# A fused adapter and layernorm on one core: the reciprocal deviation by one Heron step, squares taken from the sum, and fewer batches with b2 on the matrix engine

## The chip, the cores and the metric

The kernel runs on one core of a Trainium2 chip. The core has five engines that work side by side: TensorE (PE in the profile), VectorE (DVE), ScalarE (ACT), GpSimd (POOL) and SyncE (SP, which here only issues transfers). Each takes its instructions in the order in which they were written for it and waits for others through semaphores. The metric is the device time of one execution in microseconds; the median of three runs of the kernel before is 320.1 us (319.36 to 320.46).

## The reference, cut to what matters

The input x has 128 batches of 128 rows and 512 columns. Each batch b has a language id v (one of ten), which picks the adapter's weights and the norm's parameters. All is float32.

```python
h       = relu(x @ W1[v] + b1[v])            # 512 -> 128
adapted = h @ W2[v] + b2[v]                  # 128 -> 512
y       = x + adapted
mean    = y.mean(-1);  var = ((y - mean) ** 2).mean(-1)
out     = x + (y - mean) * rsqrt(var + 1e-5) * gamma[v] + beta[v]
```

## The kernel before, in words

All tables lie in SBUF for the whole run: the weights of all ten languages, and beta, gamma and b2, each spread over 128 partitions by a matmul at the start (`spread`, L157). For that, and for adding b2 later, the tables' 30 rows are held in bf16 as three parts that add up to the float32 value (`parts`), and a column of `pick` (L126) holds ones in the three places of one row.

One batch is one tile of 128 rows by 512 columns. It goes through these steps:

- `transpose_x` (PE, L197) and `copy_xT` (ACT, L201): x turned, by way of PSUM.
- `stage_w1` (ACT, L192): the language's W1 copied to a fixed place. `down` (PE, L220) and `relu` (ACT, L228): the hidden layer.
- `up` (PE, L237): the second product, into one of five PSUM buffers `ys[b]`. Where `b2_by_matmul(b)` holds (L187: the first four batches, and then each fourth), a bf16 matmul ahead of it (L236) puts b2[v] there first. Elsewhere `add_b2` (POOL, L207) has added b2 to x in a buffer r, one of four.
- `add_beta` (POOL, L214): x + beta into the output tile o of a pair of batches, one of five.
- `residual` (DVE, L243): y = ys + r (or + x), in PSUM; the row sums come out through DVE's accumulator, which a second small instruction reads. `negative_mean` (L248): -sum/512.
- `square` (ACT, L255): (y - mean) squared and summed. After each second batch `deviation` (L261): the square root.
- `rstd_1` to `rstd_5` (DVE, L264 to L281), once for a pair: a reciprocal of ACT's root and one Newton step for the reciprocal square root.
- `scale` (DVE, L287): (y - mean) times gamma[v], in place. `finish` (DVE, L296): times rstd, plus o. `store` (SP): 512 KB of a finished pair.

The order is written out by hand. A loop over i (L461) issues, for each engine, its steps for different batches: transposes of batch i, `down` and `relu` of i-1, `up` of i-2, `residual` of b = i-3, and `scale`, rstd steps and `finish` for the pair before b's. `keep` (L43) ties each instruction behind the one before it on its engine, so the program's order is each engine's order. The loop's body has two forms: b even (L494) and b odd (L509). On DVE, for an even b: residual, scale, negative_mean, rstd_1, rstd_2, finish, rstd_3; for an odd b: residual, rstd_4, scale, rstd_5, negative_mean, finish. Where an instruction of DVE reads what DVE has just written, it waits on DVE's own semaphore.

A language id is needed as a register where it picks a column range. `lid` (L171) loads four ids at a time on each engine; the loads of the following group are issued at the end of the loop's body (L525), for DVE behind the last `finish` of every fourth batch.

The last five batches, after E = 123, are issued by `tail` (L360), one by one instead of by pairs: `rstd_of` (L311) holds the same five steps for one batch, and `by_pool` (L342) gives three of the closing steps to ACT and POOL, for two of them with `shift` (L338, mean times rstd, on DVE) ahead. At b = E POOL gets the remaining b2 and beta additions in one go (L487).

Of the kernel before, what the change touches and what calls it, by code (L numbers as in the profile page):

```python
# [8 lines left out]
FP = mybir.dt.float32  # L9
# [7 lines left out]
P = 128  # L17
# [6 lines left out]
def cond_resid_kernel(ctx: ExitStack, tc: tile.TileContext, x, itok, W1, b1, W2, b2, gamma, beta, out):  # L24
# [102 lines left out]
    both = st.tile([P, R], FP, tag="both", name="both", bufs=1)[:96, :]  # L127
    keep(nc.vector.tensor_tensor(both, ident[:96, 0:R], ident[:96, 32 : 32 + R], ALU.add))
    keep(nc.vector.tensor_tensor(pick, both, ident[:96, 64 : 64 + R], ALU.add))


    wrap = const.tile([1, B], I32, name="wrap")
# [51 lines left out]
        return lids[g, engine][b % G]  # L184

    def b2_by_matmul(b):
        return b < 4 or b % 4 == 1  # L187

    def stage_w1(b):
        w1s[b] = wp.tile([P, KC, A], FP, tag="w1s", name=f"w1s_{b}")  # L190
# [39 lines left out]
    def up(b):  # L230
# [6 lines left out]
        keep(nc.tensor.matmul(ys[b], lhsT=hT[b], rhs=w2[:, bass.ds(v * H, H)], start=not m, stop=True))  # L237
        del hT[b]

    def residual(b):  # L240
        r = xb(b) if b2_by_matmul(b) else rs.pop(b)
        s = st.tile([P, 1], FP, tag="sum", name=f"sum_{b}")
        keep(nc.vector.scalar_tensor_tensor(ys[b], ys[b], 1.0, r, ALU.mult, ALU.add, accum_out=s))  # L243
        sums[b] = s

    def negative_mean(b):
        nmeans[b] = st.tile([P, 1], FP, tag="nmean", name=f"nmean_{b}")
        keep(nc.vector.tensor_scalar(nmeans[b], sums.pop(b), -1.0 / H, None, ALU.mult))  # L248

    def square(b):  # L250
        g, j = divmod(b, 2)
        if j == 0:
            ssqs[g] = st.tile([P, 2], FP, tag="ssq", name=f"ssq_{g}")
        sq = tp.tile([P, H], FP, tag="sq", name=f"sq_{b}")
        keep(nc.scalar.activation(sq, ys[b], AF.Square, bias=nmeans[b], accum_out=ssqs[g][:, j : j + 1]))  # L255

    sds, y0s, stats = {}, {}, {}

    def deviation(g):
        sds[g] = st.tile([P, 2], FP, tag="sd", name=f"sd_{g}")  # L260
        keep(nc.scalar.activation(sds[g], ssqs[g], AF.Sqrt, bias=eps, scale=1.0 / H))  # L261


    def rstd_1(g):  # L264
        stats[g] = p_s.tile([P, 6], FP, tag="s", name=f"stat_{g}")
        keep(nc.vector.tensor_scalar(stats[g][:, 0:2], ssqs.pop(g), -0.5 / H, -0.5 * EPS, ALU.mult, ALU.add))  # L266

    def rstd_2(g):
        y0s[g] = st.tile([P, 2], FP, tag="y0", name=f"y0_{g}")
        keep(nc.vector.reciprocal(y0s[g], sds.pop(g)))  # L270

    def rstd_3(g):
        keep(nc.vector.tensor_tensor(stats[g][:, 2:4], stats[g][:, 0:2], y0s[g], ALU.mult))  # L273

    def rstd_4(g):
        keep(nc.vector.tensor_tensor(stats[g][:, 4:6], stats[g][:, 2:4], y0s[g], ALU.mult))  # L276

    def rstd_5(g):
        rstds[g] = st.tile([P, 2], FP, tag="rstd", name=f"rstd_{g}")
        keep(  # L280
            nc.vector.scalar_tensor_tensor(rstds[g], stats.pop(g)[:, 4:6], 1.5, y0s.pop(g), ALU.add, ALU.mult)  # L281
        )

    def scale(b):
        v = lid(b, ET.DVE)
        keep(
            nc.vector.scalar_tensor_tensor(  # L287
                ys[b], ys[b], nmeans.pop(b), gamma_b[:, bass.ds(v * H, H)], ALU.add, ALU.mult
            )
        )  # L290

# [19 lines left out]
    def rstd_of(b, n):  # L311

        if not ends:
            ends["t"] = p_s.tile([P, 32], FP, tag="s", name="stat_ends")
        t = ends["t"][:, 8 * (b % 4) : 8 * (b % 4) + 3]
        if n == 1:
            keep(nc.vector.tensor_scalar(t[:, 0:1], ssqs.pop(b), -0.5 / H, -0.5 * EPS, ALU.mult, ALU.add))  # L317
        elif n == 2:
            y0s[b] = st.tile([P, 1], FP, tag="y0", name=f"y0_{b}")
            keep(nc.vector.reciprocal(y0s[b], sds.pop(b)))  # L320
        elif n < 5:
            keep(nc.vector.tensor_tensor(t[:, n - 2 : n - 1], t[:, n - 3 : n - 2], y0s[b], ALU.mult))  # L322
        else:
            rstds[b] = st.tile([P, 1], FP, tag="rstd", name=f"rstd_{b}")
            keep(nc.vector.scalar_tensor_tensor(rstds[b], t[:, 2:3], 1.5, y0s.pop(b), ALU.add, ALU.mult))  # L325

    def deviation_of(b):
        ssq = st.tile([P, 1], FP, tag="ssq", name=f"ssq_{b}")
        sq = tp.tile([P, H], FP, tag="sq", name=f"sq_{b}")
        keep(nc.scalar.activation(sq, ys[b], AF.Square, bias=nmeans[b], accum_out=ssq))  # L330
        sds[b] = st.tile([P, 1], FP, tag="sd", name=f"sd_{b}")
        keep(nc.scalar.activation(sds[b], ssq, AF.Sqrt, bias=eps, scale=1.0 / H))
        ssqs[b] = ssq

    def rstd_col(b):
# [1 line left out]

    def shift(b):  # L338
        ends[b] = st.tile([P, 1], FP, tag="shift", name=f"shift_{b}")
        keep(nc.vector.tensor_tensor(ends[b], nmeans.pop(b), rstd_col(b), ALU.mult))  # L340

    def by_pool(b, scaled):  # L342

# [16 lines left out]
    def tail(b):  # L360
        p = E // 2
        if b == E + 3:
            rstd_of(b - 2, 4)
        residual(b)
        if b == E + 1:
            rstd_1(p)
            rstd_2(p)
            negative_mean(b)
            rstd_3(p)
            scale(E - 1)  # L370
            rstd_4(p)
            rstd_5(p)
            shift(E)
            finish(E - 2)
            store(p - 1)
            deviation_of(b)
            by_pool(E, False)
        elif b == E + 2:
            negative_mean(b)
            rstd_of(b - 1, 1)  # L380
            rstd_of(b - 1, 2)
            finish_last(E - 1)
            store_last(E)
            rstd_of(b - 1, 3)
            deviation_of(b)
        elif b == E + 3:
            rstd_of(b - 2, 5)
            negative_mean(b)
            shift(b - 2)
            residual(b + 1)  # L390
            negative_mean(b + 1)
            by_pool(b - 2, False)
            store_last(b - 2)
            rstd_of(b - 1, 1)
            rstd_of(b - 1, 2)
            rstd_of(b - 1, 3)
            scale(b - 1)
            deviation_of(b)
            rstd_of(b - 1, 4)
            rstd_of(b - 1, 5)  # L400
# [6 lines left out]
            rstd_of(b + 1, 1)  # L407
            rstd_of(b + 1, 2)
            rstd_of(b, 3)
            rstd_of(b + 1, 3)  # L410
            scale(b + 1)
            rstd_of(b, 4)
            rstd_of(b + 1, 4)
            rstd_of(b, 5)
            rstd_of(b + 1, 5)
            finish_last(b)
            finish_last(b + 1)

# [42 lines left out]
    for i in range(3, B + U):  # L461
        if i < B and i % G == 0 and i // G + 3 < NG:
            load_x(i // G + 3)
        b = i - U - 1
        if i == 4:
            up(2)
        if i > 3 and on(i):
            transpose_x(i)
        if b <= E:
            add_b2(b + 2)  # L470
            add_beta(b)
        if i > 4 and on(i - 1):
# [12 lines left out]
        p = g - 1  # L485
        mine, old = 0 <= p < B // 2, 0 <= p - 1 < B // 2
        if b == E:  # L487
            for n in range(b + 3, B):
                add_b2(n)
            for n in range(b + 1, B):  # L490
                add_beta(n)
        if b > E:
            tail(b)
        elif half == 0:  # L494
            if on(b):
                residual(b)
            if mine:
                scale(2 * p)
            if on(b):
                negative_mean(b)  # L500
            if mine:
                rstd_1(p)
                rstd_2(p)
            if old:
                finish(2 * p - 1)
                store(p - 1)
            if mine:
                rstd_3(p)
        else:  # L509
            if on(b):  # L510
                residual(b)
            if mine:
                rstd_4(p)
                scale(2 * p + 1)
                rstd_5(p)
# [49 lines left out]
```

## Time and profile before

| | |
|---|---|
| median of three runs | 320.1 us |
| profiled execution: its time, its span | 319.72, 318.0 us |
| granted clock of TensorE | 0.99 |
| PE, DVE, ACT, POOL busy | 302.7, 297.9, 289.1, 280.6 us |
| batches with b2 by matmul (L236) | 35, 0.38 us each |
| additions on POOL: b2 (L207), beta (L214) | 93, 128; 1.28 us each |
| scale (L287), finish (L296), residual (L243) on DVE | 0.75, 0.74, 0.69 us each |
| one rstd step (L266, L270, L273, L276, L281) | 0.15 to 0.21 us, 62 of most |

The span is the time from the first to the last instruction of the profiled execution. Instructions of an engine overlap: the next can start before the one in front has put away its last results. So in a timeline the distance from one start to the next tells what an instruction costs its engine, and the duration tells when others can use its result. The ends of matmuls are modelled, and a busy PE is not PE at its peak; there too the distances between starts are what is read.

### The profile page before, as it was taken

How to read it: one execution, taken by the hardware profiler on the slowest of the kernel's cores; microseconds unless marked ns; L12 is line 12 of the kernel's file. 1: busy time of each engine (PE TensorE's matmuls, PEld its weight loads, DVE VectorE, ACT ScalarE, POOL GpSimd, SP SyncE). 2: the span in 40 equal slices, each digit the busy share in tenths (PEclk: the TensorE clock that was granted, in tenths of full speed). 3: DMA queues.
4: the chain of work that ended last, by engine and by line, in shares of the span. 5: the costliest groups of instructions: out<-in, count | busy, mean ns of one | idle time of the engine just before them, and what ended most of it. 6: DMA issues, size and time to landing. Idle time of an engine off the chain costs nothing. (4 is left out here: it accounts for less than half of the span.)

```text
span 318.0 us, 7173 instructions
## 1 busy us (share of the span) xinstructions
PE 302.7 (95%) x1883; PEld 225.0 (71%) x1884; DVE 297.9 (94%) x995; ACT 289.1 (91%) x726; POOL 280.6 (88%) x234
## 2 busy tenths in 40 slices
PE   7989999999999999999999999999999999999950
PEld 3566777777777777777777777777777777777730
DVE  6827999999999999999999999999999999999995
ACT  3977999999999999999999999999999999999971
POOL 1308999999999999999999999999999999999873
PEclk9999999999999999999999999999999999999995
DMA  7998777667776666677776666677766666633333
GB/s 204 318 386 294 205 260 262 233 232 266 260 242 212 215 223 242 228 238 265 261 231 215 209 227 248 223 245 264 258 220 208 222 231 241 219 128 133 132 128 138
DMA packets 41002, 72.88 MB, mean 229 GB/s; under 512 B 1753, under 2 KB 6884, under 8 KB 40962
## 3 DMA queue, kind: packets, MB, share of 16 engines
q1 hardware_dynamic: 40902, 72.38, 67.2%
q8 instruction: 15, 0.25, 0.3%
q14 instruction: 25, 0.20, 0.2%
q10 hardware_dynamic: 60, 0.05, 0.1%
HBM read 38.86 MB, written 33.55 MB: 228 GB/s over the span
## 5 line engine op out<-in xcount | busy, mean ns | idle before, releaser
L214 POOL TENSOR_TENSOR o<-x,beta_b 128x512 f32<-128x512 f32 x128 | 162.1, 1280 | 9.2 <-ACT beta_b L164 9.2
L207 POOL TENSOR_TENSOR r<-x,b_b 128x512 f32<-128x512 f32 x93 | 118.9, 1279 | 20.2 <-DMA x<-in_x_dram 12.3
L220 PE MATMUL ph<-xT,w1s 128*128 128x128 f32 x1024 | 135.6, 275 | 0.7 <-ACT w1s L192 0.5
L237 PE MATMUL py<-w,hT 128*128 x256 | 131.0, 594 | 0.9 <-DMA w<-in_L_cond_W_dram 0.7
L220 PEld LDWEIGHTS ph<-xT,w1s 128*128 128x128 f32 x1024 | 124.6, 192 | 2.8 <-ACT hT L228 1.4
L197 PEld LDWEIGHTS pxT<-ident,x 128*128 128x128 f32 x512 | 63.7, 140 | 66.1 <-issue 45.3
L287 DVE SCALAR_TENSOR_TENSOR py<-py,nmean,gamma_b 128x512 f32<-128x512 f32 x126 | 94.6, 751 | 0.0
L255 ACT ACTIVATE sq<-py,nmean 128x512 f32<-128x512 f32 x124 | 85.3, 688 | 6.7 <-DVE nmean L248 4.2
L296 DVE SCALAR_TENSOR_TENSOR o<-py,rstd,o 128x512 f32<-128x512 f32 x122 | 90.3, 740 | 1.0
L192 ACT COPY w1s<-w 128x512 f32 x128 | 79.5, 622 | 0.2 <-DMA w<-in_L_cond_W_dram 0.2
L201 ACT COPY xT<-pxT 128x512 f32<-128x512 f32 x128 | 73.8, 577 | 5.1 <-PE pxT L197 3.6
L197 PE MATMUL pxT<-ident,x 128*128 128x128 f32 x512 | 76.8, 273 | 0.7 <-ACT xT L201 0.7
L243 DVE SCALAR_TENSOR_TENSOR py<-py,r 128x512 f32<-128x512 f32 x93 | 64.4, 692 | 2.5 <-PE pxT L197 0.9
L228 ACT ACTIVATE hT<-ph,b1T 128x128 f32<-128x128 f32 x128 | 47.6, 372 | 1.2 <-PE ph L220 1.2
L237 PEld LDWEIGHTS py<-w,hT 128*128 128x128 f32 x256 | 41.6, 192 | 4.0 <-issue 2.0
L243 DVE SCALAR_TENSOR_TENSOR py<-py,x 128x512 f32<-128x512 f32 x35 | 24.1, 690 | 4.9 <-PE py L237 4.8
L255 ACT ACTIVATION_READ_ACCUMULATOR sq<-py,nmean 128x1 f32 x124 | 24.8, 200 | 0.0
L261 ACT ACTIVATE sd<-ssq,eps 128x2 f32<-128x2 f32 x62 | 18.3, 296 | 2.1
L248 DVE TENSOR_SCALAR nmean<-sum 128x1 f32<-128x1 f32 x128 | 18.7, 146 | 0.2
L236 PE MATMUL py<-parts,pick 96*128 96x512 bf16 x35 | 13.3, 381 | 0.0
L243 DVE DVE_READ_ACCUMULATOR py<-py,r 128x1 f32 x93 | 13.0, 140 | 0.0
L276 DVE TENSOR_TENSOR stat<-stat,y 128x2 f32<-128x2 f32 x62 | 12.7, 205 | 0.0
(54 smaller groups left out, 113.7 us busy)
## 6 DMA issues: line engine op xcount, KB each, us to landing
out_dram<-o SPq DMA_DIRECT2D x61, 512.0 KB, 3.6
x<-in_x_dram SPq DMA_DIRECT2D x30, 1024.0 KB, 6.0
w<-in_L_cond_W_dram SPq DMA_DIRECT2D x4, 640.0 KB, 6.6
w<-in_L_cond_W_dram SPq DMA_DIRECT2D x2, 1280.0 KB, 11.3
x<-in_x_dram SPq DMA_DIRECT2D x4, 512.0 KB, 8.5
out_dram<-o SPq DMA_DIRECT2D x6, 256.0 KB, 2.4
rows<-in_L_cond_beta_dram ACTq DMA_DIRECT2D x1, 20.0 KB
rows<-in_L_cond_gamma_dram SPq DMA_DIRECT2D x1, 20.0 KB
```

The source lines that it names most:

```text
L192: keep(nc.scalar.copy(w1s[b].rearrange("p k a -> p (k a)"), src))
L197: keep(nc.tensor.transpose(pxs[b][:, k, :], xb(b)[:, k * P : (k + 1) * P], ident))
L201: keep(nc.scalar.copy(xT[b], pxs.pop(b)))
L207: keep(nc.gpsimd.tensor_tensor(rs[b], xb(b), b2_b[:, bass.ds(v * H, H)], ALU.add))
L214: keep(nc.gpsimd.tensor_tensor(os[g][:, j, :], xb(b), beta_b[:, bass.ds(v * H, H)], ALU.add))
L220: nc.tensor.matmul(phs[b], lhsT=w1s[b][:, k, :], rhs=xT[b][:, k, :], start=(k == 0), stop=(k == KC - 1))
L228: keep(nc.scalar.activation(hT[b], phs.pop(b), AF.Relu, bias=b1T[:, bass.ds(lid(b, ET.Activation), 1)]))
L237: keep(nc.tensor.matmul(ys[b], lhsT=hT[b], rhs=w2[:, bass.ds(v * H, H)], start=not m, stop=True))
L243: keep(nc.vector.scalar_tensor_tensor(ys[b], ys[b], 1.0, r, ALU.mult, ALU.add, accum_out=s))
L255: keep(nc.scalar.activation(sq, ys[b], AF.Square, bias=nmeans[b], accum_out=ssqs[g][:, j : j + 1]))
L287: nc.vector.scalar_tensor_tensor(ys[b], ys[b], nmeans.pop(b), gamma_b[:, bass.ds(v * H, H)], ALU.add, ALU.mult)
L296: nc.vector.scalar_tensor_tensor(o, ys.pop(b), rstds[g][:, j : j + 1], o, ALU.mult, ALU.add)
```

## The change

Four things are changed together.

- **Heron's step.** With s the root from ACT and a the exact variance plus eps, the kernel now forms s + a/s, which is twice the improved root, and takes its reciprocal. That is four DVE instructions for a pair instead of five: reciprocal, (ssq + eps) times it, that plus s, reciprocal. The result is half of the reciprocal deviation, so gamma's columns of `pick` are doubled once at the start, and with them the spread gamma.
- **Square from the sum.** `square` takes the row sum as its bias and -512 as its scale, so that it squares sum - 512 y, which is 512 times the distance from the mean. It reads `sums` and no longer `nmeans`; the constants 1/512^3 take the factors out again. Sums and negative means lie in tiles of two columns, one pair each.
- **b2 by matmul** in the first four batches and then in batches 1, 6 and 11 of each sixteen, instead of each fourth: 27 batches instead of 35. The other 8 are added on POOL.
- **Order on DVE.** For an even b: residual, scale, rstd_1, negative_mean, rstd_2, finish, rstd_3. For an odd b: residual, rstd_4, negative_mean, scale, finish. The tail is arranged anew, and in POOL's last block the addition of b2 to the last batch moves behind the beta additions.

```diff
+    keep(nc.vector.tensor_scalar(pick[:, L : 2 * L], pick[:, L : 2 * L], 2.0, None, ALU.mult))
...
-        return b < 4 or b % 4 == 1
+        return b < 4 or b % 16 in (1, 6, 11)
...
+    def col(tiles, b):
+
+        return tiles[b // 2][:, b % 2 : b % 2 + 1]
+
     def residual(b):
         r = xb(b) if b2_by_matmul(b) else rs.pop(b)
-        s = st.tile([P, 1], FP, tag="sum", name=f"sum_{b}")
-        keep(nc.vector.scalar_tensor_tensor(ys[b], ys[b], 1.0, r, ALU.mult, ALU.add, accum_out=s))
-        sums[b] = s
+        if b % 2 == 0:
+            sums[b // 2] = st.tile([P, 2], FP, tag="sum", name=f"sum_{b // 2}")
+        keep(
+            nc.vector.scalar_tensor_tensor(ys[b], ys[b], 1.0, r, ALU.mult, ALU.add, accum_out=col(sums, b))
+        )
...
-        keep(nc.scalar.activation(sq, ys[b], AF.Square, bias=nmeans[b], accum_out=ssqs[g][:, j : j + 1]))
+        keep(
+            nc.scalar.activation(
+                sq, ys[b], AF.Square, bias=col(sums, b), scale=-float(H), accum_out=col(ssqs, b)
+            )
+        )
...
+    H3 = float(H) ** 3
...
-        keep(nc.scalar.activation(sds[g], ssqs[g], AF.Sqrt, bias=eps, scale=1.0 / H))
+        keep(nc.scalar.activation(sds[g], ssqs[g], AF.Sqrt, bias=eps, scale=1.0 / H3))
...
     def rstd_1(g):
-        stats[g] = p_s.tile([P, 6], FP, tag="s", name=f"stat_{g}")
-        keep(nc.vector.tensor_scalar(stats[g][:, 0:2], ssqs.pop(g), -0.5 / H, -0.5 * EPS, ALU.mult, ALU.add))
+        y0s[g] = p_s.tile([P, 6], FP, tag="s", name=f"stat_{g}")
+        keep(nc.vector.reciprocal(y0s[g][:, 0:2], sds[g]))
 
     def rstd_2(g):
-        y0s[g] = st.tile([P, 2], FP, tag="y0", name=f"y0_{g}")
-        keep(nc.vector.reciprocal(y0s[g], sds.pop(g)))
+        t = y0s[g]
+        keep(nc.vector.scalar_tensor_tensor(t[:, 2:4], ssqs.pop(g), EPS * H3, t[:, 0:2], ALU.add, ALU.mult))
 
     def rstd_3(g):
-        keep(nc.vector.tensor_tensor(stats[g][:, 2:4], stats[g][:, 0:2], y0s[g], ALU.mult))
+        t = y0s[g]
+        keep(nc.vector.scalar_tensor_tensor(t[:, 4:6], t[:, 2:4], 1.0 / H3, sds.pop(g), ALU.mult, ALU.add))
 
     def rstd_4(g):
-        keep(nc.vector.tensor_tensor(stats[g][:, 4:6], stats[g][:, 2:4], y0s[g], ALU.mult))
-
-    def rstd_5(g):
         rstds[g] = st.tile([P, 2], FP, tag="rstd", name=f"rstd_{g}")
-        keep(
-            nc.vector.scalar_tensor_tensor(rstds[g], stats.pop(g)[:, 4:6], 1.5, y0s.pop(g), ALU.add, ALU.mult)
-        )
+        keep(nc.vector.reciprocal(rstds[g], y0s.pop(g)[:, 4:6]))
...
         if b == E:
-            for n in range(b + 3, B):
-                add_b2(n)
+            add_b2(b + 3)
             for n in range(b + 1, B):
                 add_beta(n)
+            add_b2(b + 4)
...
             if mine:
                 scale(2 * p)
+                rstd_1(p)
             if on(b):
                 negative_mean(b)
             if mine:
-                rstd_1(p)
                 rstd_2(p)
...
             if mine:
                 rstd_4(p)
-                scale(2 * p + 1)
-                rstd_5(p)
             if on(b):
                 negative_mean(b)
             if mine:
+                scale(2 * p + 1)
                 finish(2 * p)
```

`rstd_of` for single batches changes in the same way. In `tail`, the four steps take the places of the five, with negative_mean moved between the reciprocal and the step that reads it, and the third and fourth steps of batch 124 around residual(126).

More of the change, by code (lines that the diff above doesn't have):

```diff
@@ L238, in up @@
         del hT[b]
+    def col(tiles, b):
+        return tiles[b // 2][:, b % 2 : b % 2 + 1]
     def residual(b):
         r = xb(b) if b2_by_matmul(b) else rs.pop(b)
-        s = st.tile([P, 1], FP, tag="sum", name=f"sum_{b}")
-        keep(nc.vector.scalar_tensor_tensor(ys[b], ys[b], 1.0, r, ALU.mult, ALU.add, accum_out=s))
-        sums[b] = s
+        if b % 2 == 0:
[3 more added lines that the diff above has]
+        )
     def negative_mean(b):
-        nmeans[b] = st.tile([P, 1], FP, tag="nmean", name=f"nmean_{b}")
-        keep(nc.vector.tensor_scalar(nmeans[b], sums.pop(b), -1.0 / H, None, ALU.mult))
+        if b % 2 == 0:
+            nmeans[b // 2] = st.tile([P, 2], FP, tag="nmean", name=f"nmean_{b // 2}")
+        keep(nc.vector.tensor_scalar(col(nmeans, b), col(sums, b), -1.0 / H, None, ALU.mult))
     def square(b):
@@ L287, in scale @@
             nc.vector.scalar_tensor_tensor(
-                ys[b], ys[b], nmeans.pop(b), gamma_b[:, bass.ds(v * H, H)], ALU.add, ALU.mult
+                ys[b], ys[b], col(nmeans, b), gamma_b[:, bass.ds(v * H, H)], ALU.add, ALU.mult
             )
@@ L316, in rstd_of @@
         if n == 1:
-            keep(nc.vector.tensor_scalar(t[:, 0:1], ssqs.pop(b), -0.5 / H, -0.5 * EPS, ALU.mult, ALU.add))
+            keep(nc.vector.reciprocal(t[:, 0:1], sds[b]))
         elif n == 2:
[L319 to L322, printed above, removed]
+            keep(
+                nc.vector.scalar_tensor_tensor(t[:, 1:2], ssqs.pop(b), EPS * H3, t[:, 0:1], ALU.add, ALU.mult)
+            )
+        elif n == 3:
+            keep(nc.vector.scalar_tensor_tensor(t[:, 2:3], t[:, 1:2], 1.0 / H3, sds.pop(b), ALU.mult, ALU.add))
         else:
             rstds[b] = st.tile([P, 1], FP, tag="rstd", name=f"rstd_{b}")
-            keep(nc.vector.scalar_tensor_tensor(rstds[b], t[:, 2:3], 1.5, y0s.pop(b), ALU.add, ALU.mult))
+            keep(nc.vector.reciprocal(rstds[b], t[:, 2:3]))
     def deviation_of(b):
@@ L329, in deviation_of @@
         sq = tp.tile([P, H], FP, tag="sq", name=f"sq_{b}")
-        keep(nc.scalar.activation(sq, ys[b], AF.Square, bias=nmeans[b], accum_out=ssq))
+        keep(nc.scalar.activation(sq, ys[b], AF.Square, bias=col(sums, b), scale=-float(H), accum_out=ssq))
         sds[b] = st.tile([P, 1], FP, tag="sd", name=f"sd_{b}")
-        keep(nc.scalar.activation(sds[b], ssq, AF.Sqrt, bias=eps, scale=1.0 / H))
+        keep(nc.scalar.activation(sds[b], ssq, AF.Sqrt, bias=eps, scale=1.0 / H3))
         ssqs[b] = ssq
@@ L339, in shift @@
         ends[b] = st.tile([P, 1], FP, tag="shift", name=f"shift_{b}")
-        keep(nc.vector.tensor_tensor(ends[b], nmeans.pop(b), rstd_col(b), ALU.mult))
+        keep(nc.vector.tensor_tensor(ends[b], col(nmeans, b), rstd_col(b), ALU.mult))
     def by_pool(b, scaled):
@@ L362, in tail @@
         if b == E + 3:
-            rstd_of(b - 2, 4)
+            rstd_of(b - 2, 3)
         residual(b)
@@ L366, in tail @@
             rstd_1(p)
+            negative_mean(b)
             rstd_2(p)
-            negative_mean(b)
+            scale(E - 1)
             rstd_3(p)
-            scale(E - 1)
             rstd_4(p)
-            rstd_5(p)
             shift(E)
@@ L378, in tail @@
         elif b == E + 2:
+            rstd_of(b - 1, 1)
             negative_mean(b)
-            rstd_of(b - 1, 1)
             rstd_of(b - 1, 2)
@@ L383, in tail @@
             store_last(E)
-            rstd_of(b - 1, 3)
             deviation_of(b)
         elif b == E + 3:
-            rstd_of(b - 2, 5)
-            negative_mean(b)
+            rstd_of(b - 2, 4)
             shift(b - 2)
             residual(b + 1)
-            negative_mean(b + 1)
             by_pool(b - 2, False)
@@ L394, in tail @@
             rstd_of(b - 1, 1)
+            negative_mean(b)
             rstd_of(b - 1, 2)
-            rstd_of(b - 1, 3)
+            negative_mean(b + 1)
             scale(b - 1)
             deviation_of(b)
+            rstd_of(b - 1, 3)
             rstd_of(b - 1, 4)
-            rstd_of(b - 1, 5)
             scale(b)
@@ L407, in tail @@
             rstd_of(b + 1, 1)
+            rstd_of(b, 3)
             rstd_of(b + 1, 2)
-            rstd_of(b, 3)
-            rstd_of(b + 1, 3)
             scale(b + 1)
             rstd_of(b, 4)
+            rstd_of(b + 1, 3)
             rstd_of(b + 1, 4)
-            rstd_of(b, 5)
-            rstd_of(b + 1, 5)
             finish_last(b)
@@ L513, in cond_resid_kernel @@
                 rstd_4(p)
-                scale(2 * p + 1)
-                rstd_5(p)
             if on(b):
```

## The prediction

> **What bounds the kernel now.** First the page's busy table and the sums of three stretches of the span:
>
> ```profile
> PE 302.7 (95%) x1883; PEld 225.0 (71%) x1884; DVE 297.9 (94%) x995; ACT 289.1 (91%) x726; POOL 280.6 (88%) x234
> ```
>
> ```profile
> 30.00:300.00 270.00, 270.00 (x1715) 205.25 (x1714) 266.42 (x901) 259.42 (x661) 262.06 (x213) 1.00 0.66 225
> ```
>
> Four engines lie within 4% of the stretch's length, so shares don't settle it; PE's is modelled too. What settles it is the rhythm, in PE's timeline:
>
> ```profile
> 155.44 0.60 PE L197 MATMUL pxT<-ident,x 128*128 128x128 f32 x4
> ...
> 157.63 0.60 PE L197 MATMUL pxT<-ident,x 128*128 128x128 f32 x4
> 158.07 1.06 PE L220 MATMUL ph<-xT,w1s 128*128 128x128 f32 x8
> 158.96 0.38 PE L236 MATMUL py<-parts,pick 96*128 96x512 bf16 x1
> 159.18 1.02 PE L237 MATMUL py<-w,hT 128*128 x2
> 160.04 0.60 PE L197 MATMUL pxT<-ident,x 128*128 128x128 f32 x4
> ```
>
> A batch takes 2.19 us from transpose to transpose (155.44 to 157.63), and 2.41 with a b2 matmul (157.63 to 160.04): 0.22 each. Four batches take 8.98, unbroken from 31 to 301 us: PE sets the pace. DVE's timeline shows how near it is:
>
> ```profile
> 153.72 0.69 DVE L243 SCALAR_TENSOR_TENSOR py<-py,r 128x512 f32<-128x512 f32 x1
> ...
> 154.99 0.15 DVE L248 TENSOR_SCALAR nmean<-sum 128x1 f32<-128x1 f32 x1
> 155.05 0.15 DVE L266 TENSOR_SCALAR stat<-ssq 128x2 f32<-128x2 f32 x1
> 155.11 0.15 DVE L270 RECIPROCAL y<-sd 128x2 f32<-128x2 f32 x1
> 155.18 0.73 DVE L296 SCALAR_TENSOR_TENSOR o<-py,rstd,o 128x512 f32<-128x512 f32 x1
> ...
> 155.89 0.69 DVE L243 SCALAR_TENSOR_TENSOR py<-py,r 128x512 f32<-128x512 f32 x1
> ...
> 157.42 0.75 DVE L296 SCALAR_TENSOR_TENSOR o<-py,rstd,o 128x512 f32<-128x512 f32 x1
> 158.22 0.70 DVE L243 SCALAR_TENSOR_TENSOR py<-py,r 128x512 f32<-128x512 f32 x1
> ```
>
> One pair (153.72 to 158.22) takes 4.50; the pair before (149.28 to 153.72) 4.44; together 8.94 against PE's 8.98. DVE's bound is 0.5% away. Small operations last 0.15 but follow each other at 0.06 to 0.07. The finish at 157.42 is followed by residual after 0.80, the one at 153.05 after 0.67. At the first place, once in four batches, stands the loading of the next four language ids into registers (L174). It takes no engine time, but DVE's instructions are handed out behind it. The answer by source line gives its length:
>
> ```profile
> L174 DVEq TENSOR_LOAD <-lang x32: 341/612/1049, 24.6 to 301.0; - x32
> ```
>
> The finish in front of it waits for rstd_5, so finish is handed out only when it can start, and the load starts with it. Finish alone would let residual go after 0.66; the load makes it 0.80, sticking out by 0.14. Where it took 1.05, at 49.26, residual came 1.23 after finish.
>
> [...] the ids are loaded while a finish handed out before runs on[...]. [...] Here such a wait costs: a reader starts 0.19 after the small writer's start (308.69 to 308.88 in the tail), not 0.07. [...] shift (L340), at 303.82, lasts 0.46, till POOL's additions end at 304.26.
>
> **The change part by part** (durations of the profiled execution: span 318.0, its time 319.72, 0.4 below the median of 320.1).
>
> *PE.* Picks fall from 35 to 27. Seven of the eight lie before residual(124): 7 x 0.22 = 1.54 off PE; batch 125 in the tail is the eighth. PE's four batches become 4 x 2.19 + 0.75 x 0.22 = 8.925.
>
> *POOL* takes 8 additions, at 1.23 start to start: +9.9. Sixteen batches need (13 + 16) x 1.23 = 35.7, PE 35.7. But POOL runs ahead: r_4 ends at 26.6 and its residual starts at 31.95, 5.3 later. The one addition that batch 5 now needs costs some 1.2 of this, later ones only keep POOL from gaining. Work on path: nil. Without the lead, 9.9 would appear. x buffers are freed later by the 2 to 4 us of lead that POOL lacks, and SP's queue holds its loads, and the stores behind them, as much longer. The load of group 8 is issued at 63.61, needs 6.0, and its first transpose is at 88.19: 18 us hide it. If that were gone, transposes would wait for x.
>
> *DVE, first half of a pair.* Now nmean, rstd_1, rstd_2, finish take 0.19 (154.99 to 155.18). New: reciprocal, nmean, rstd_2, which reads the reciprocal's result: 0.19 of waiting plus 0.07 to finish = 0.26. Loss 0.065, in both pairs 0.13 per four batches. Behind the waiting rstd_2 stand finish, rstd_3 and the next residual, and for that residual ACT's square waits, with 2 us of room until its deviation is used.
>
> *DVE, second half.* nmean now stands directly behind residual and rstd_4 and must wait for the accumulator. In the tail the same step is 308.39 (accumulator read) to 308.56: 0.17. scale stands behind it with its register instruction; the same pattern 308.88 to 309.01 is 0.13. So residual to finish: 0.61 + 0.17 + 0.13 + 0.67 = 1.58, against 1.53 (155.89 to 157.42) and 1.59 (151.46 to 153.05): loss 0.04. rstd_5 and its wait are gone from this place.
>
> *DVE, the ids.* finish now waits for rstd_4, written before scale, so it enters the queue while scale runs, and the load behind it can start some 0.65 earlier. Its excess vanishes; finish to residual becomes 0.66: -0.14 in one pair and -0.01 in the other, and another -0.01 for a residual that already stands in the queue. From scale's start to finish's end are 1.3 us: even a load of 1.05 nearly fits.
>
> Sum: 0.13 + 0.04 - 0.16 = 0.01: DVE stays at about 8.945, and is now just above PE's 8.925. Residual(3) starts at 29.68, PE-fed as today; residual(124) at 301.73: 272.05 for 121 batches. After: 30.25 x 8.945 = 270.6. Three long loads cost DVE 0.48, 0.41 and 0.39 today (at 50.47, 59.77 and 230.26, together 1.3), which its small lead over PE pays back; with no such lead I keep 0.5 of it: 271.1. Gain 1.0.
>
> *ACT.* square needs the sum only: 4.2 of waits for nmean are taken from an engine with 3% of room; nothing on the path. sqrt has equal form and cost.
>
> *Front.* One more small operation on pick, before DVE's wait of 0.4 for rows: hidden.
>
> *Tail*, DVE's own: residual(124) to the last pair of finishes is 301.73 to 313.11 = 11.38. One of the five rstd steps goes for each of five batches (two pairs and single ones), which is worth 0.07 where it was covered and 0.19 where the next one read it. Against that, both shifts, with two SBUF inputs, can be held by POOL, which now works on its additions until about 25.35 + 227 x 1.232 = 305.0 instead of 304.3. Between 10.6 (steps gained, 4 x 0.19) and 11.8 (nothing gained but a shift held 0.4 longer): I take 10.9, gain 0.5. The last r_127, at the end of POOL's block, is ready by 305; residual(127) wants it at about 306.5.
>
> Total -1.5: 320.1 - 1.5 = 318.6.
>
> Unknowns, both ends: the ids' load, -0.15 to 0 per four batches (0 = +4.2 on the sum); the two waits, 0.02 more or less each, four times per four batches: +-2.4; the tail, -0.8 to +0.4.
>
> **Rivals.** *PE alone decides*: DVE's waits are each 0.01 to 0.02 cheaper. Then 1.54 + tail 0.8 + the start: 317.4 to 317.8. For it: PE's floor is only 0.02 below; against: DVE's waits were measured.
>
> *The new waits eat it all*: DVE at 8.98 per four, 0.01 more per wait; 30.25 x 8.98 + 0.5 = 272.1; tail 0: 320.1. For it: the margin is thin; against: the long loads lose their exposed part.
>
> *Slower: the ids' load stays exposed.* If the sequencer can't pass finish before the engine takes it, 0.14 per four batches remains: 30.25 x 0.14 = 4.2, so 318.6 + 4.2 = 322.8. It decides from 0.05 per four batches on. For it: today every load starts with a finish; against: at 24.65 a load ran behind a small instruction and no finish at all, and today's finish is handed out late because it waits for rstd_5, a cause that goes.
>
> *Slower: POOL.* At 1.28 start to start instead of 1.23 it needs 37.1 per sixteen batches, 1.3 more than DVE, 10 in all, less its lead of 5: 323 to 325. Against: 1.23 was held through the whole catching-up at 31 to 100 us.
>
> **How the numbers follow.** As summed (317.9 to 319.1) 0.46; PE alone 0.14; nothing left (within 0.3%, about what a measurement of this kernel can tell from none, so 319.1 to 321.1) 0.22; ids' load 0.12; POOL 0.06. Faster 0.60, same 0.22, slower 0.18. The range, 317.2 to 321.3, leaves out the two slow rivals and the edge of the PE case. The likeliest case alone is 317.9 to 319.1.
>
> **What would show it.** Right: transposes 2.19 and 2.41 as before, but with waits of PE for DVE's finish (L309 of the new kernel) in the middle; four batches at 8.93 to 8.96; every finish followed by residual at 0.65 to 0.67, ids' loads beginning during scale; reciprocal to rstd_2 0.19; residual to finish 1.58. Wrong: residual waiting for POOL's r; loads still starting with finish; four batches above 8.98; or residual to finish well off 1.58.

## The result and the profile after

The changed kernel takes 330.84 us (median of six runs, 330.49 to 331.53), against 320.1 before: 1.0343 times as long, with an interval of 1.0326 to 1.036. The prediction was 318.6, with a range of 317.2 to 321.3. The profiled execution took 330.74 us, its span is 329.0. Ratios and intervals, here and below, are from undisturbed executions; one kernel of the experiments, the one before with the new picks and kept stores, ran some 2% longer in five of its eight executions, for a reason that stays open, and is read by the other three. First the page's busy table of the changed kernel, and the sums of the same long stretch of its span (the last three columns are TensorE's granted clock, the DMA share and GB/s):

```profile
PE 305.1 (93%) x1876; PEld 224.7 (68%) x1876; DVE 308.8 (94%) x930; ACT 288.1 (88%) x726; POOL 289.6 (88%) x242
```

```profile
30.00:300.00 270.00, 268.49 (x1693) 202.93 (x1692) 267.09 (x831) 256.07 (x656) 259.11 (x211) 1.00 0.65 224
```

The table says little. PE is busy 2.4 us more though it has eight matmuls less; DVE is busy 10.9 us more though it has 65 instructions less, mostly because the table counts an operation that is held up as busy (7.96 of the shift below). In the long stretch POOL is busy 2.95 us *less* than before (262.06), although it was given more to do. The landmarks in DVE's timeline tell more:

| | before | predicted | after |
|---|---|---|---|
| residual(3) starts | 29.68 | as before | 30.02 |
| DVE, four batches | 8.94 | 8.945 | 9.01 |
| residual(124) starts | 301.73 | 300.8 | 305.19 |
| from there to the last finishes | 11.38 | 10.9 | 19.39 |
| from there to the end of the span | 4.9 | | 4.4 |

The span grew by 11.0 us: 3.5 had come by residual(124), 8.0 came between it and the last finishes, and 0.5 was won back behind them. DVE's timeline in the middle, from the steps of one batch to the residual of the batch after the next, shows the steps that the change was about:

```profile
155.57 0.17 DVE L283 RECIPROCAL stat<-sd 128x2 f32<-128x2 f32 x1
...
155.85 0.74 DVE L309 SCALAR_TENSOR_TENSOR o<-py,rstd,o 128x512 f32<-128x512 f32 x1
...
156.57 0.69 DVE L251 SCALAR_TENSOR_TENSOR py<-py,x 128x512 f32<-128x512 f32 x1
...
158.15 0.74 DVE L309 SCALAR_TENSOR_TENSOR o<-py,rstd,o 128x512 f32<-128x512 f32 x1
158.81 0.69 DVE L251 SCALAR_TENSOR_TENSOR py<-py,r 128x512 f32<-128x512 f32 x1
```

From residual (156.57) to finish (158.15) it is 1.58, and from finish to the next residual 0.66, with no trace of the ids' load: both as predicted. From reciprocal (155.57) to finish (155.85) it is 0.28, and 0.27 in the pair before, where 0.26 was predicted. The chain of waits names what is new, and none of it is in these steps:

```profile
POOL o L216 <- DMA out_dram<-o: 10.9, 7, 1.7
...
PE py L239 <- DVE o L309: 10.1, 3, 8.6
ACT n L360 <- DVE shift L354: 9.7, 2, 8.2
...
DVE py L251 <- POOL r L209: 2.0, 2, 1.1
```

The columns are the waiting engine, its tile and line, what it waited for, microseconds in all, times, and the longest. POOL waits seven times for an output tile until the store of its former contents has landed; before, it never did. ACT waits 8.2 us for one shift, and PE 8.6 for a finish that stands behind that shift on DVE. DVE's timeline has the shift, which computes one column of results:

```profile
307.24 7.96 DVE L354 TENSOR_TENSOR shift<-nmean,rstd 128x1 f32<-128x1 f32 x1
```

And POOL's timeline of the same time:

```profile
309.04 4.91 POOL L216 TENSOR_TENSOR o<-x,beta_b 128x512 f32<-128x512 f32 x4
313.91 1.26 POOL L209 TENSOR_TENSOR r<-x,b_b 128x512 f32<-128x512 f32 x1
```

The shift ends when POOL's unbroken block of additions ends, at 315.17. Before, the same two stood like this:

```profile
303.82 0.46 DVE L340 TENSOR_TENSOR shift<-nmean,rstd 128x1 f32<-128x1 f32 x1
299.30 4.96 POOL L214 TENSOR_TENSOR o<-x,beta_b 128x512 f32<-128x512 f32 x4
```

The block ended at 304.26 and held the shift for a few tenths only. Two things have happened: POOL's block came 11 us later, and the shift could not get past it.

The granted clock doesn't explain the loss up to here: from 30 to 300 us it is 1.00 in both kernels. It falls in the tail, behind the hold. PE stands idle for 8.56 us until 315.90; from 315 to 320 its granted clock is 0.50, where before, from 305 to 310, it was 1.00. Before, it fell as well once PE had no more to do, behind its last matmuls (305.00 to 306.98): 0.65 from 310 to 315, 0.50 from 315 to 318. The last four matmuls of `up` take 3.78 us there, against 1.98 before, and DVE waits 0.58 and 0.73 for them. So some 1.3 of the 8.0 us came by way of PE.

### Why POOL came late

The queue's own timeline (SyncE, SPq: only issues of transfers; xN counts neighbours of one kind) of the kernel before:

```profile
98.53 0.38 SPq L67 DMA_DIRECT2D x<-in_x_dram  x1
102.19 4.88 SPq L300 DMA_DIRECT2D out_dram<-o  x2
107.46 0.38 SPq L67 DMA_DIRECT2D x<-in_x_dram  x1
```

and of the changed kernel:

```profile
103.98 0.38 SPq L67 DMA_DIRECT2D x<-in_x_dram  x1
104.45 2.64 SPq L313 DMA_DIRECT2D out_dram<-o  x2
112.60 0.38 SPq L67 DMA_DIRECT2D x<-in_x_dram  x1
113.07 7.53 SPq L313 DMA_DIRECT2D out_dram<-o  x3
121.23 9.00 SPq L67 DMA_DIRECT2D x<-in_x_dram  x2
130.72 3.74 SPq L313 DMA_DIRECT2D out_dram<-o  x3
```

Before, one load is followed by two stores, throughout: the order in which they are written. After, the order is another: three stores, two loads, three stores. The same with names, numbered by counting the transfers of the two timelines from their beginning (x_8 is a group of four batches, o_7 a pair):

```
before: x_8 o_7 o_8 x_9 o_9 o_10 x_10 o_11 o_12 x_11 o_13 o_14 ...
after:  x_9 o_9 o_10 o_11 x_10 x_11 o_12 o_13 o_14 x_12 o_15 o_16 x_13 o_17 o_18 o_19 x_14 x_15 o_20 ...
```

Once in each sixteen batches two loads stand side by side: of the written order x_10, o_11, o_12, x_11, the store o_11 has moved ahead of its load, and o_12 behind the next one. The second load waits for one of four buffers of x that POOL still reads, and the stores wait behind it, though their data are ready. One such place in SyncE's timeline:

```profile
196.08 9.00 SPq L67 DMA_DIRECT2D x<-in_x_dram  x2
205.17 1.94 SPq L313 DMA_DIRECT2D out_dram<-o  x3
```

The first of these stores is, by the same count, o_36. DVE's timeline has the finish that completes this pair:

```profile
196.40 0.74 DVE L309 SCALAR_TENSOR_TENSOR o<-py,rstd,o 128x512 f32<-128x512 f32 x1
```

The pair is ready at 197.14, and its store is issued 8.0 us later. SyncE's waits show how long it stands in all, before:

```profile
SPq L300 <- DVE stat L273: 217.0, 60, 4.6
...
SPq L67 <- POOL o L214: 8.1, 6, 2.7
```

and after:

```profile
SPq L67 <- POOL o L216: 133.1, 26, 8.9
SPq L313 <- DVE stat L291: 78.7, 28, 5.3
```

Before, SyncE mostly waits in front of a store for DVE, which is harmless; a load held it 8.1 us for POOL in the whole run. After, loads hold it 133.1 us. Stores, now mostly issued right behind a load of 1 MB (103.98 and 104.45), land after a median of 7.2 us instead of 3.6. So an output tile is late once in sixteen batches, and POOL, which has no tile to write, stands. Behind the store of 205.17 it is this addition:

```profile
212.37 1.29 POOL L216 TENSOR_TENSOR o<-x,beta_b 128x512 f32<-128x512 f32 x1 [1.54 <-DMA out_dram<-o]
```

Such gaps stand at 62.89, 100.21, 137.66, 175.05, 212.37, 249.71 and 286.89, about 37.4 apart: sixteen batches at POOL's own pace (29 additions at 1.23 = 35.7) and one gap. In 37.4 us DVE, at 9.01 for four batches, does more than sixteen. The lead of r over its residual falls from 7.2 us at batch 19 to 5.2 at batch 21, and so in steps to nothing at batch 101, where DVE first waits for r (its residual starts at 252.24). And a late POOL frees x late, which holds the next load longer.

### The profile page after: what moved, and what is told of

It reads as the page before. It is cut to its first block, busy times and chain, and to the rows that moved or that the text cites. A ratio compares the mean times of both kernels' runs of the same rounds, so it can differ in the third digit from the quotient of the medians.

```text
span 329.0 us, 7090 instructions
## 1 busy us (share of the span) xinstructions
PE 305.1 (93%) x1876; PEld 224.7 (68%) x1876; DVE 308.8 (94%) x930; ACT 288.1 (88%) x726; POOL 289.6 (88%) x242
## 4 chain that ended last, share of the span: by engine, by line
PE 65%; POOL 10%; issue 8%; DVE 7%; DMA 3%; SPq 3%; DVEq 1%; POOLq 1%; ACT 0%
PE py L239 27%; PE ph L222 25%; PE pxT L199 12%; POOL o L216 5%; POOL r L209 5%; DMA w<-in_L_cond_W_dram 3%; DVE py L251 3%; SPq L98 2%; DVE py L300 2%; PE py L238 1%; DVE o L309 1%; SPq L84 1%; DVEq L176 1%; POOLq L176 1%; DVE nmean L257 0%
## 5 line engine op out<-in xcount | busy, mean ns | idle before, releaser
L216 POOL TENSOR_TENSOR o<-x,beta_b 128x512 f32<-128x512 f32 x128 | 163.2, 1286 | 20.0 <-DMA out_dram<-o 10.9
L239 PE MATMUL py<-w,hT 128*128 x256 | 134.7, 609 | 10.8 <-DVE o L309 10.1
L209 POOL TENSOR_TENSOR r<-x,b_b 128x512 f32<-128x512 f32 x101 | 130.1, 1288 | 11.3 <-DMA x<-in_x_dram 11.3
L266 ACT ACTIVATE sq<-py,sum 128x512 f32<-128x512 f32 x124 | 85.3, 688 | 4.2 <-DVE rstd L295 2.1
L251 DVE SCALAR_TENSOR_TENSOR py<-py,r 128x512 f32<-128x512 f32 x101 | 69.8, 691 | 3.6 <-POOL r L209 2.0
L239 PEld LDWEIGHTS py<-w,hT 128*128 128x128 f32 x256 | 40.5, 192 | 15.7 <-DVE o L309 10.6
L266 ACT ACTIVATION_READ_ACCUMULATOR sq<-py,sum 128x1 f32 x124 | 25.3, 204 | 0.0
L251 DVE SCALAR_TENSOR_TENSOR py<-py,x 128x512 f32<-128x512 f32 x27 | 18.7, 692 | 4.6 <-PE py L239 4.6
L251 DVE DVE_READ_ACCUMULATOR py<-py,r 128x1 f32 x101 | 14.4, 143 | 0.0
L283 DVE RECIPROCAL stat<-sd 128x2 f32<-128x2 f32 x62 | 10.2, 165 | 0.5 <-ACT sd L277 0.5
L295 DVE RECIPROCAL rstd<-stat 128x2 f32<-128x2 f32 x62 | 10.4, 167 | 0.0
```

The lines of the kernel that those rows point to most:

```text
L209: keep(nc.gpsimd.tensor_tensor(rs[b], xb(b), b2_b[:, bass.ds(v * H, H)], ALU.add))
L216: keep(nc.gpsimd.tensor_tensor(os[g][:, j, :], xb(b), beta_b[:, bass.ds(v * H, H)], ALU.add))
L266: nc.scalar.activation(sq, ys[b], AF.Square, bias=col(sums, b), scale=-float(H), accum_out=col(ssqs, b))
```

## The experiments

Theory A is what the last section says: the stores' place in SyncE's queue costs POOL its lead, and then its block holds the shift. Theory B: the eight more additions are simply too many for POOL, whatever the queue does. Theory C: DVE's new steps cause the loss. Expectations that mean something else by a letter say so.

### The changed kernel with the old picks

```diff
-        return b < 4 or b % 16 in (1, 6, 11)
+        return b < 4 or b % 4 == 1
```

> The changed kernel, but with b2 by matmul in each fourth batch again (35 picks); Heron, the square and the order stay. Theory A (GpSimd's lead is lost to the store queue, and shift is then held by its additions): the lead of GpSimd stays at 9 us or more, shift lasts under 0.6, VectorE still takes 9.01 per four batches, so residual(124) at 30.0 + 30.25 x 9.01 = 302.6 and about 320 in all (319.3 to 321). Rival B (GpSimd's 8 more additions of 1.23 are simply 9.9 us too many): also about 320. Rival C (VectorE's new steps and waits cause the loss): stays above 328.

320.25 us, 1.0015 (1.0 to 1.003). All that was rewritten on DVE and ACT costs at most 0.3%. SyncE's order is that of the kernel before, POOL waits for no store, its block ends at 303.89, the shifts last 0.16 and 0.52. DVE takes 9.01 for four batches here too, so that is its own new pace; the tail (residual(124) at 302.97 to the last finishes at 313.44) takes 10.47. C falls as the main cause.

### The kernel before with the new picks alone

```diff
-        return b < 4 or b % 4 == 1
+        return b < 4 or b % 16 in (1, 6, 11)
```

> The kernel before with nothing changed but the picks (27 instead of 35). Theory A: GpSimd starts with the same smaller lead, loads of x wait for it in SyncE's queue, stores behind them are late, GpSimd waits some 10 us for output tiles, shift is held for several us: 326 to 331. Rival B: 330. Rival C: 318 to 319, since TensorE is 1.5 us shorter and VectorE as before.

332.27 us, 1.0392 (1.0364 to 1.0419), 1.3 us beyond the expected 331. This one line carries the whole loss. The chain of waits is that of the changed kernel:

```profile
POOL o L214 <- DMA out_dram<-o: 11.3, 7, 1.7
...
ACT n L346 <- DVE shift L340: 9.4, 2, 8.1
```

It does not yet tell A from B: both need the picks.

### The load of x written two batches later

```diff
-        if i < B and i % G == 0 and i // G + 3 < NG:
-            load_x(i // G + 3)
...
+        if i < B and i % G == 2 and i // G + 3 < NG:
+            load_x(i // G + 3)
```

(The first is at the loop's start, the second at the end of its body.)

> The changed kernel, with each load of an x group issued two batches later, behind the stores that stood behind it. GpSimd's work is the same. Theory A: no waits of GpSimd for output tiles (10.9 before), lead at the end 5 us or more, shift under 1.3, residual(124) at 302.6: 319.3 to 321.5. Rival B: 329 to 331, as GpSimd has as much to do. Rival C: 329 to 331.

331.45 us, 1.036 (1.0328 to 1.0392): no help, the expectation missed. SyncE's timeline says why:

```profile
104.45 0.38 SPq L67 DMA_DIRECT2D x<-in_x_dram  x1
104.92 1.77 SPq L313 DMA_DIRECT2D out_dram<-o  x2
```

The order and nearly the times are those of the changed kernel. So the place where a transfer is written doesn't alone fix where it stands. `load_x` is under `keep`, which ties loads to loads; `store` (L311 to L313) is not, so a store may pass loads when the program is put in order. My edit had moved nothing.

### Stores tied to their written place

```diff
-        nc.sync.dma_start(out=out[2 * g : 2 * g + 2].rearrange("b s h -> s b h"), in_=os.pop(g))
+        keep(nc.sync.dma_start(out=out[2 * g : 2 * g + 2].rearrange("b s h -> s b h"), in_=os.pop(g)))
```

> The changed kernel with its picks, but the stores tied into the written order of SyncE's queue, so that each load of x stands where the loop puts it: load, store, store, as in the kernel before. Theory A' (the new picks made the scheduler put two loads of x side by side in each sixteen batches, the second ahead of two stores; the stores wait, then GpSimd waits for output tiles, then shift for GpSimd): no wait of GpSimd for output tiles, lead of r and o kept, shift held at most 1 us, residual(124) at about 303.0, 319.6 to 320.8. Rival B (8 more additions are too many for GpSimd): 329 to 331. Rival C (SyncE's order of the scheduler is a bystander): 330.8.

322.0 us, 1.0078 (1.0057 to 1.01). POOL does the same work as in the changed kernel, and more than three quarters of the loss are gone (1.0343 before the edit). B falls as the main cause. SyncE's timeline has one load and two stores in turn again:

```profile
100.67 0.38 SPq L67 DMA_DIRECT2D x<-in_x_dram  x1
101.92 4.87 SPq L313 DMA_DIRECT2D out_dram<-o  x2
109.42 0.38 SPq L67 DMA_DIRECT2D x<-in_x_dram  x1
```

POOL waits for a store only twice (2.4 us in all), and its block ends at 307.0. Against the expected 319.6 to 320.8 it misses by 1.2: the block is still there when the shift comes, at 305.15, and holds it 1.86.

### The shift with one input from SBUF as a tile

The same product, with rstd as a scalar pointer instead of a second tile:

```diff
-        keep(nc.vector.tensor_tensor(ends[b], col(nmeans, b), rstd_col(b), ALU.mult))
+        keep(nc.vector.tensor_scalar(ends[b], col(nmeans, b), rstd_col(b), None, ALU.mult))
```

First in the changed kernel, with its stores where they were:

> The changed kernel, with shift computed by a tensor_scalar that takes rstd as its per-partition scalar, so that it has one SBUF tensor input instead of two. Theory A: shift lasts 0.2 instead of 7.96, and VectorE goes on at 307.4; GpSimd's last additions still end at 315.2, and residual(127), which wants the last of them, starts there instead of at 319.8: about 326 (325 to 327.5). Rival B: 329 to 331, since GpSimd ends no earlier. Rival C: 330.8, no change.

328.3 us, 1.0256 (1.0232 to 1.0281). The shift takes 0.21 with POOL at work beside it, so it was POOL's block that held it and not anything DVE waits for. But only 2.5 us of the 8 come back, 0.8 short of the expected range, for the next thing in line is late as well. DVE's timeline at residual(127):

```profile
315.60 0.70 DVE L251 SCALAR_TENSOR_TENSOR py<-py,r 128x512 f32<-128x512 f32 x1 [4.53 <-POOL r L209]
```

The last r comes from the end of POOL's block, 315.56. With POOL that late, the hold only hid a wait. And of the 4.2 us by which DVE's last finishes start earlier (320.38 for 324.58), 1.7 are lost at the end, where SyncE's last stores wait up to 9.2 us for POOL. Then with the stores kept as well:

> The changed kernel with two mends: stores kept in their written place, and the shift as an operation with one tile input and a pointer; DVE's order is left as the change has it. With stores kept alone: residual(124) 303.12, then 12.17 to the last finish but one, of which the two shifts took 2.41. Theory A [...]: residual(124) about 303.1, shifts 0.2 each, 10.5 to the last finish but one as in the run with the old picks, so about 313.6; time 320.0 to 320.8, that is about the kernel before. Rival (the last b2 addition at the end of POOL's block sets the tail): residual(127) waits for r, ready at about 307, and the time stays at 321 to 322.

320.36 us, 1.0013 (0.9996 to 1.0029). Shifts of 0.21, residual(124) at 303.13, the last finishes at 313.32, as expected. With these two edits, neither of which touches the arithmetic, the change costs nothing measurable: A explains the loss.

### The kernel before with the new picks and kept stores

```diff
-        return b < 4 or b % 4 == 1
+        return b < 4 or b % 16 in (1, 6, 11)
...
-        nc.sync.dma_start(out=out[2 * g : 2 * g + 2].rearrange("b s h -> s b h"), in_=os.pop(g))
+        keep(nc.sync.dma_start(out=out[2 * g : 2 * g + 2].rearrange("b s h -> s b h"), in_=os.pop(g)))
```

> The kernel before with the new picks alone and the stores tied into the written order. Theory A': the 12 us of the picks alone go; TensorE at 8.925 and VectorE at 8.943 per four batches give residual(124) at about 301.0; shift, now at 303.1, is held till GpSimd's additions end at about 305, a us more than before: 319 to 321. Rival B: 330 or more.

320.42 to 321.51 us, 1.0035 (0.9999 to 1.007), against 1.0392 with the stores free. The longest of all its executions, 328.23, is still below the shortest with the stores free, 332.21. The kept stores mend the loss without any of the new steps on DVE.

### DVE's order, with the stores kept

In the changed kernel three operations start 0.12 to 0.18 behind the one in front of them, where others start 0.07 behind: rstd_2, negative_mean and scale. Here the large `scale` is put in between: rstd_1 stands in front of it, and in the odd half it stands between rstd_4 and negative_mean.

```diff
             if mine:
-                scale(2 * p)
                 rstd_1(p)
+                scale(2 * p)
...
                 rstd_4(p)
+                scale(2 * p + 1)
             if on(b):
                 negative_mean(b)
             if mine:
-                scale(2 * p + 1)
                 finish(2 * p)
```

> As e5_stores_kept, and VectorE's order changed: rstd_1 ahead of scale in the first half of a pair, negative_mean behind scale in the second, so that neither reader stands right behind its writer. Theory A' with the step prices read from the trace: VectorE's own work falls from 9.01 to about 8.52 per four batches, TensorE decides again at 8.925, residual(124) at about 300.2; but shift then starts at 302.3 and is held till GpSimd's additions end at about 305: 319.2 to 320.3. If the waits cost nothing (rival): as e5.

319.93 us, 1.0007 (0.9994 to 1.0019). DVE is now ahead of PE: residual follows finish after 0.78 and 0.86 (151.60 to 152.38, 156.12 to 156.98) instead of 0.66. Four batches take PE's 8.98 three times and 8.76 the fourth time, and residual(124) comes at 299.80. But an earlier DVE meets more of POOL's block: the shift starts at 301.86 and is held 3.48 us, to 305.34, with the block ending at 305.32. With the shift's edit added:

> As e7_stores_kept_vector_order, with shift as a tensor_scalar of one SBUF tensor input. Theory A': shift lasts 0.2, the tail has no hold: residual(124) at 300.2, last finish 10.5 later: 316.6 to 317.8, below both kernels. Rival B (GpSimd decides the end whatever holds shift): as e7.

318.31 us, 0.9945 (0.993 to 0.9959): 0.4 to 0.7% faster than the kernel before, though 0.5 us above the expected 317.8.

### What the fewer picks are worth

The last version, with the old picks again:

> The version with stores kept in their written place, the new order on DVE and the shift with one tile input, but with b2 by TensorE in each fourth batch again, as before the change (35 instead of 27). It tells what the fewer picks are worth once nothing they cost stands in the way. Theory A (with stores in place and DVE's order shortened PE sets the pace, so each pick taken away is worth its 0.22): four batches 8.98 throughout instead of 8.76 in one of four, so residual(124) 1.5 later than with the new picks, at about 301.9; POOL's additions end at about 304; time 319.2 to 319.9. Rival P (the picks buy nothing in any arrangement, the end is set by DVE or POOL): residual(124) about 300.3 and 318.3, within 0.3.

318.48 us, 0.9963 (0.9949 to 0.9976). Neither theory: from residual(3) to residual(124) it takes 271.70 where the new picks took 270.18, so each pick is worth its 0.22 on PE; but the end is the same. The last line of POOL's timeline with the new picks:

```profile
309.62 2.48 POOL L364 TENSOR_TENSOR o<-n,o 128x512 f32<-128x512 f32 x2
```

and with the old ones:

```profile
309.30 2.48 POOL L364 TENSOR_TENSOR o<-n,o 128x512 f32<-128x512 f32 x2
```

DVE's last pair of finishes starts 1.1 earlier with the new picks (310.56, 311.70), but POOL ends 0.3 later, at 312.10. The three last stores stand in SyncE's queue behind each other, and the first of them waits for POOL: the last is issued at 313.04, against 313.12 with the old picks. So POOL's end takes the gain back, or most of it: the two intervals overlap, and they were not measured side by side. The test is to take two b2 additions from POOL's last block, in batches 126 and 127, and to run it beside the version without:

```diff
-        return b < 4 or b % 16 in (1, 6, 11)
+        return b < 4 or b % 16 in (1, 6, 11) or b > 125
```

> The best version so far (new picks, stores kept, new order on DVE, shift with one tile input), with b2 by TensorE in batches 126 and 127 as well, so that POOL has two additions less in its last block, 2.5 us. It tells whether POOL's end sets the end of the version without this. Theory Q (it does: there POOL ended at 312.1, after DVE's last finish, and the stores of the last two batches were issued one by one behind a store that waits for POOL, the last at 313.0; with the old picks POOL ended at 311.8 though DVE ended 1.1 later, so the 1.5 that the fewer picks gain on PE were lost there): POOL's additions end at about 303.3, its last operation at about 310.6, the last store is issued at about 312.0, and the time is 0.7 to 1.1 less than that of the same kernel without the two, run beside it: 317.2 to 317.6. Rival (DVE's end or the 0.44 of PE's two matmuls decides): no difference, or up to 0.4 slower.

> The best version so far once more, unchanged, beside the one with two b2 additions less at the end, so that both are measured on one chip. It took 318.31 us, 0.9945 of the kernel before. Theory: 318.3 within 0.4 again, and 0.7 to 1.1 above the run beside it.

316.46 us, 0.9888 (0.9867 to 0.9909), with the two matmuls, and 317.56, 0.992 (0.9903 to 0.9937), without: 1.1 less, at the upper edge of what was expected. Both times are lower than expected: the version without came out 0.75 below its earlier 318.31. With the two, POOL ends at 310.17, the last store is issued at 311.53; without, POOL ends at 311.09 and the store goes at 312.02.

## Why the prediction was wrong

**The step that failed** is "POOL", in its sentence on x: "SP's queue holds its loads, and the stores behind them, as much longer", priced at nothing because "18 us hide it". The 18 us are the cover of a load. For a store no cover was named, and who waits for a store was not asked: POOL does, for one of five output tiles. And the sentence took the queue's order to be what it was before. The description ahead of the prediction says that the program's order is each engine's order; that holds for what stands under `keep`, and `store` doesn't. The prediction followed the change through the order on DVE, ACT and POOL; for SyncE it kept the order of the kernel before. So "Work on path: nil" became 10.9 us of waiting on POOL, its lead of some 7 us was spent, and 2.0 us of it reached DVE before the tail. What moved one store ahead of its load and the next one behind the second load, with no other edit than the picks, stays open: the profile shows the order, not its reasons.

**"Tail"**: "a shift held 0.4 longer" was the most that was allowed. It took 7.96. What holds the shift, POOL's block, was named rightly, from the one hold of 0.46 before, and sized by the block's predicted end at 305.0, which came at 315.17. Between "nothing gained but a shift held 0.4 longer" and what happened lies the same wrong input. With POOL in time, in the changed kernel with the old picks, the tail took 10.47, a little below the lower bound of 10.6 to 11.8. From there to 19.39, the hold makes 7.8 and DVE's two waits for PE, at half its clock, 1.3.

**"DVE, first half"** was mis-sized: from residual to residual it took 2.26 to 2.27 against 2.17 before, a loss of 0.09 to 0.10 instead of 0.065, in both pairs. Some 0.015 is in reciprocal to finish (0.275 for 0.26), the rest in the steps around finish (0.72 to 0.73 from finish to the next residual, 0.71 before). That makes 9.01 for four batches instead of 8.945, or 30.25 x 0.065 = 2.0 us. The unknown's bound of plus 2.4 covered it. **"DVE, second half"** (1.58) and **"the ids"** (0.66 behind finish, with loads of 340 to 994 ns that, after the first, start 0.07 to 0.17 behind the start of scale) were right.

**"PE"** was right in its price (0.22 a pick, 1.5 in all, shown where the last version runs with the old and the new picks) and wrong in thinking it reachable: DVE at 9.01 never let PE's 8.925 show.

**"POOL pace"** as a rival (1.28) was wrong in cause, since POOL kept 1.23 (204.60 to 205.83), but it was the only case that let POOL lose its lead. Its 323 to 325 left out what a late POOL does to the tail. Sum of what was not foreseen, against the predicted time for residual(124), 300.8: start 0.3, pace 2.0, DVE's waits for r 2.0 and some 0.1 of others make 305.2; then 19.39 - 10.9 = 8.5 in the tail. Two of the signs of being wrong came: residual waited for r, and four batches took more than 8.98. The 0.5 kept for long loads was used up: one load stuck out by 0.26, at 122.8, and the rest is in smaller ones.

## What to carry to other kernels

A change that gives an engine more work is to be followed into the buffers that this engine takes and frees, and into the order of the transfer queue as it is built, from its first row to its last: a store that is not tied can change its place, and one load that waits in front of it makes everybody downstream late (here SyncE stood up to 8.9 us in front of one load, and POOL 10.9 us in all for stores). A lead is a stock that a small, regular loss empties: 1.5 us in each 37 took three quarters of the kernel to show (the first wait for r is at 252), and then cost 8 us at one place. And when a stall is removed, look at what is late right behind it before counting the gain.

## What the runs showed of the hardware

The shift, a DVE operation with two inputs from SBUF, takes 0.16 us where POOL stands (at 318.90 in the changed kernel). In these four kernels it was held until POOL's whole unbroken row of additions had ended, not just one of them:

| kernel | shift starts | lasts | shift ends | POOL's block ends |
|---|---|---|---|---|
| changed | 307.24 | 7.96 | 315.20 | 315.17 |
| before with new picks | 308.30 | 8.01 | 316.31 | 316.29 |
| stores kept | 305.15 | 1.86 | 307.01 | 307.00 |
| stores kept, DVE's order | 301.86 | 3.48 | 305.34 | 305.32 |

In all four it ends 0.01 to 0.03 us behind the row's last addition. POOL's additions follow each other at some 1.22 us there, and in the changed kernel six of them started (307.82 to 313.91) while the shift stood. The small step at 306.84 in the same kernel, with one of its two inputs in PSUM, took 0.16 beside POOL's addition of 306.60. The shift's product with one SBUF tile and a scalar pointer took 0.21 beside a busy POOL: from 307.62 on, in the changed kernel with that edit alone, and from 305.17 on with the stores kept as well, where one addition runs from 304.11 to 305.41. By what POOL holds such an operation, no run here shows.
